# A planned graph-network kernel: layer jobs without order between units, the last two groups in alternation, and shifted ranks

## The chip, the cores and the metric

The kernel runs on one core of a Trainium2 chip. The core has a matrix engine (TensorE, PE in the profile), a vector engine (VectorE, DVE), an engine for activation functions (ScalarE, ACT), a general engine (GpSimd, POOL) and an engine that here only issues transfers (SyncE, SP). Each works through its own queue of instructions strictly in order, and an instruction waits at the head of its queue until what it needs has been signalled.

The metric is the device time of one execution in microseconds (us), as the median of several runs. Lower is better.

## What is computed

The input is 128 graphs of 64 nodes with 256 features, `x`, an integer adjacency `adj`, and a node mask of ones. Four layers follow, each of the form `x = x + layer(relu(layernorm(x)), adj)`:

```python
# 0: graph attention, 4 heads of 64:  softmax over neighbours of leaky_relu(e_src + e_dst), then elu
x = x + _L0_gnn_ref(h, adj, ...)
# 1: the same with one head of 256
x = x + _L1_gnn_ref(h, adj, ...)
# 2: relations: sum over r of (adj == r) @ ((h W + b_r) * sigmoid(h W Wg + bg_r)), then relu
x = x + _L2_gnn_ref(h, nodemask, adj, ...)
# 3: gated recurrence, three times:
m = h @ weight[i];  aggr = A^T @ m;  h = gru_cell(aggr, h)     # A = (adj != 0)
```

With edges of 0 and 1 only one of layer 2's relations can occur. The kernel computes this case in its fast part and sets a flag from the largest edge; a general part, which is not run on these inputs, stands behind that flag. All arithmetic is in 32-bit floating point. A layer of the recurrence consists of the sum over neighbours, the products for the two gates and for the candidate, `tanh` for each of them, and the new state `(1 - z) n + z h`.

## The kernel before

**Tiling.** Two graphs make one tile of 128 nodes, and four tiles make a group (`G = 4`), so there are 16 groups (`NG`). A group goes through layer 0, 1 and 2 (`first_layer`, `second_layer`, `third_layer`), and then through three steps of the recurrence. Groups 0 and 1 go through the three layers as two units of two tiles each, the other groups as one unit. In the recurrence, the state is held with features on partitions (`hT`), as two halves of 128 features (c = 0, 1), and each step multiplies it by a recursive scheme of seven products in place of eight (`Sevens`), with sums of the state (`hS`) and of the neighbour sums (`aS`) made on GpSimd. A step has 42 products of 128 by 128 by 256, each carried out in two passes of the matrix engine. The neighbour sum itself (`along`) needs the state with nodes on partitions (`hnat`) and is made of 64 by 64 products that run beside each other.

**From a step to the next.** The new state `hT` must be turned back into `hnat`. There are two ways. `back` transposes on TensorE and copies on ScalarE: this is used when the next step in the list is of the same group (`quick`), and for the last step of all (`final`). Otherwise `back_by_dma` transposes blocks of 32 on VectorE, writes them to DRAM in one transfer (tile `way`), and reads them back with four transfers; for a group's last step, `finish` then adds the result to `xg` on GpSimd and stores it.

**The order of the steps.** The list `steps` (line 1486) interleaves neighbouring groups: (g, 0), (g-1, 2), (g, 1) for each g, where (g, i) is step i of group g. It ends with (14,0), (13,2), (14,1), (15,0), (14,2), (15,1), (15,2). `when` gives every step a time slot of 27 us, from which due times of the jobs are taken, and two places ahead of a group's first step `enter` records its three layers.

**The planner.** Nothing is emitted as it is written. While `nc.on` is set, every call is recorded as an `Op` of a `Job`, with a cost from a formula (`cost`, line 529) and its dependences. `Plan.emit` (line 462) then lays all of them out in time, `PASSES` times: `forward` goes ahead in time and always takes the operation that can start earliest, or of those within a leeway the one of the lowest rank (`op.due`), on each engine; `backward` goes back from the end, and its latest starts become the ranks of the next pass, with a little noise from `SEED`. The order of the pass with the earliest end is emitted, and so becomes the order of the five queues. A job with names in `after` may not start before these jobs have ended (line 368). Buffers are taken from pools at plan time as they come free.

**Jobs that wait for jobs.** In `layers_of`, the dictionary `users` (line 1495) holds for each of the three layers the last unit that was recorded in it, and the next unit's job of that layer names it in `after` (line 1514): layer i of a unit waits for the whole of layer i of the unit before.

**Fillers.** Before the planned time of 115 us, `emit` puts matmuls on a constant tile (`warm`, line 1579) where it has planned TensorE to be idle, one for each 220 ns, as long as no bank of the recurrence has been used. Their results are not used.

**A step's end.** In `step` (line 1005), `gates` makes r and z for each c, `from_h` and `from_a` make the candidate. Each of r, z and the candidate comes in two halves of 256 columns (h = 0, 1). `z_there` applies the `tanh` to z of one c when both halves are there, and `done` makes the new state of that c in two operations of 512 columns. The last step of all is called with `in_parts`: its results are stored in three pieces.

Of the kernel before, what the change touches and what calls it, by code (L numbers as in the profile page):

```python
# [2 lines left out]

# [8 lines left out]
AF = mybir.ActivationFunctionType  # L12
# [209 lines left out]
class Plan:  # L222
# [54 lines left out]
            b.ops.append(op)  # L277
        return op

    PASSES, SEED, SPREAD = 21, 28, 50.0  # L280
    LEEWAY = {"PE": 100.0, "DVE": 100.0, "Activation": 100.0, "Pool": 100.0, "SP": 300.0, "-": 0.0}
    OVERLAP = {"DVE": 83.0, "Activation": 95.0, "Pool": 43.0}
    ISSUE, TURN = 665.0, 197.0
# [133 lines left out]
    def backward(self, end):  # L417
# [19 lines left out]
        def limit(op, late):  # L437
            if late < op.late:
                op.late = late
            op.waits -= 1  # L440
            if not op.waits:
                ready[op.engine].append(op)

        for _ in self.ops:
# [14 lines left out]
            for other in before[op]:  # L459
                limit(other, op.due - self.LATENCY - other.took)  # L460

    def emit(self):

        self.on = False
        self.link()
        best, self.random = None, Random(self.SEED)
        for _ in range(self.PASSES):
            end, order = self.forward()
            if best is None or end < best[0]:
                best = end, [(op, op.start, op.idle, op.places) for op in order]  # L470
            self.backward(end)
        self.ends = best[0]
        for op, start, idle, places in best[1]:
            op.start = start
            if op.engine == "PE" and self.spare and start < 115.0 * 1e3:
                for _ in range(int((idle - 100.0) / 220.0)):
                    self.spare()
            for b, tag in places:
                b.pool.make(b, tag)
            op.call()  # L480
        self.ops = []
        return best[0]
# [26 lines left out]
def elements(x):  # L509
    n = 1  # L510
    for k in x.shape[1:]:
        n *= k
    return n
# [15 lines left out]
def cost(engine, method, args, kwargs):  # L529

    n = elements(args[0])
    if engine == "tensor":
        m = elements(args[2] if method == "matmul" else args[0])
        return (m / 1.2 + 2.5) * (1 if method == "transpose" else 2)
    if engine == "sync" or method == "dma_start":
        to, of = args[:2]
        rate = {"way": 450.0, "fine": 175.0}.get(to.base.tag, 150.0) if isinstance(to, View) else 150.0
        if isinstance(of, View) and of.base.tag in ("way", "fine"):
            rate = 150.0 if of.base.tag == "way" else 100.0
        return n * to.shape[0] * 4 / rate  # L540
    if engine == "vector":
        if method == "bn_stats":
            return 400.0
        if method == "tensor_reduce":
            n = elements(args[1])
        plain = method == "tensor_scalar" and not any(isinstance(a, View) for a in args[2:4])
        return 150.0 + n * (0.53 if plain and n >= 512 else 1.04)
    if engine == "scalar":
        return 150.0 + 0.86 * n if method in ("copy", "mul") else 310.0 + 0.73 * n
    if ALU.pow in args:  # L550
        return 1000.0
    return 200.0 + 2.1 * n if method != "memset" else 100.0 + 0.85 * n
# [3 lines left out]
def kernel(  # L556
# [28 lines left out]
    nc = Plan(tc.nc)  # L585
    B = x.shape[0]
    NP = B * N // P
    NG = NP // G
# [26 lines left out]
    brz = nc.kept(const, [P, 4], F32, name="brz")  # L615

    def state(work, plain, name="hT"):

        return work.tile([P, K, G, P] if plain else [P, P // S, K, G * S], F32, name=name)

    def chunk(x, k):

        return x[:, k] if x.shape[1] == K else x[:, :, k]
# [301 lines left out]
    class Recurrence:  # L925
# [7 lines left out]
        def at(self, x, k, h):  # L933

            return chunk(x, k)[:, 2 * h : 2 * h + 2]
# [69 lines left out]
        def step(self, i, back=True, in_parts=False):  # L1005
# [4 lines left out]
            at = self.at  # L1010
# [45 lines left out]
            hnew = state(work, self.plain)  # L1056
            t = [[at(hnew, c, h) for h in range(2)] for c in range(K)]

            def turned_part(name):
                return work.tile([P, P // S, P], F32, name=name)  # L1060
# [18 lines left out]
            def gates(c):  # L1079
                g = Sevens(c, "r", (0, 1))  # L1080
                rs, zs = (turned_part(name) for name in "rz")
                r, z = ([x[:, 2 * h : 2 * h + 2] for h in range(2)] for x in (rs, zs))

                def r_there(h, y):
                    nc.scalar.activation(r[h], y, AF.Tanh, bias=brz[:, c : c + 1], scale=0.5)
                    nc.vector.scalar_tensor_tensor(t[c][h], r[h], 1.0, t[c][h], op0=ALU.add, op1=ALU.mult)

                def z_there(h, y):
                    nc.vector.tensor_tensor(z[h], y, z[h], ALU.add)
                    if h == 0:  # L1090
                        nc.scalar.activation(zs, zs, AF.Tanh, bias=brz[:, 2 + c : 3 + c], scale=0.5)

                nc.scalar.copy(r[0], g.mul("y", 1))
                nc.vector.tensor_tensor(r[0], g.mul("m", 2), r[0], ALU.add)
                r_there(0, r[0])
                nc.scalar.copy(z[0], g.mul("y", 6))
                nc.scalar.copy(z[1], g.mul("y", 5))
                z_there(1, g.mul("z", 7))
                r_there(1, g.mul("y", 3))
                z_there(0, g.mul("z", 4))  # L1100
                return r, z, rs, zs

            def done(d, z, to):
                nc.vector.scalar_tensor_tensor(d, z, 1.0, d, op0=ALU.add, op1=ALU.mult)
                nc.vector.scalar_tensor_tensor(to, d, 0.5, to, op0=ALU.mult, op1=ALU.add)

            def from_a(gated):
                n = Sevens(0, "n", (1,))

                def add(c, h, y):  # L1110
                    nc.vector.tensor_tensor(t[c][h], t[c][h], y, ALU.add)

                def there(c, h):
                    d, z, ds, zs = gated[c]
                    nc.scalar.activation(t[c][h], t[c][h], AF.Tanh, bias=bi[:, 4 + c : 5 + c])
                    nc.gpsimd.tensor_tensor(d[h], at(hT, c, h), t[c][h], ALU.subtract)

                add(0, 0, n.mul("y", 1))
                add(0, 0, n.mul("m", 2))
                there(0, 0)  # L1120
                add(1, 0, n.mul("y", 6))
                add(1, 1, n.mul("y", 5))
                add(1, 1, n.mul("z", 7))
                there(1, 1)
                add(0, 1, n.mul("y", 3))
                there(0, 1)
                done(*gated[0][2:], chunk(hnew, 0))
                if back:
                    back_first()
                add(1, 0, n.mul("z", 4))  # L1130
                there(1, 0)
                done(*gated[1][2:], chunk(hnew, 1))

            def back_first():
                self.hT = hnew
# [23 lines left out]
    with ExitStack() as s1:  # L1159
# [126 lines left out]
        for s in range(2):  # L1286
            h = slice(s * N, (s + 1) * N)
# [196 lines left out]
        start, slot = 87.96, 27.0  # L1484
        PLAIN = (0, NG - 1)
        steps = [(0, 0), (0, 1)]
        for g in range(1, NG):
            steps += [(g, 0), (g - 1, 2), (g, 1)]
        steps.append((NG - 1, 2))
        turn = {step: n for n, step in enumerate(steps)}  # L1490

        def when(g, i):
            return start + turn[g, i] * slot

        users = {}

        def layers_of(g):
            if g > 1:
                load_group(g)

            if g == 0:
                units = [(0, 2, (-2.5, 24.3, 61.4, 71.1)), (2, 2, (-2.7, 25.3, 58.8, 74.4))]
            elif g == 1:
                units = [(0, 2, (24.1, 54.4, 87.6, 97.3)), (2, 2, (45.5, 67.3, 90.0, 120.0))]
            elif g == 2:
                units = [(0, G, (74.5, 115.0, 160.0, 205.0))]
            else:
                end = when(g, 0) - 32.8
                units = [(0, G, [end - 51.3 * i + x for i, x in ((3, 0.0), (2, -0.95), (1, -4.68), (0, 0.0))])]
            for p0, n, at in units:  # L1510
                spare = g == 0 and p0 > 0
                for i in range(3):
                    end = None if g < 2 else at[i + 1]
                    nc.begin((g, p0, i), at[i], end, [users[i]] if i in users and not spare else [])
                    if g > 1:
                        nc.job.spread = 3.0
                    if not spare:
                        users[i] = (g, p0, i)
                    layers[i](g, p0, n, spare)
            if g == 0:  # L1520
                nc.begin("make")
                nc.note("-", make_gru, 0.0, [], [], [op for op in nc.ops if any(b.pool is early for b in op.bases)])
# [12 lines left out]
        for n, (g, i) in enumerate(steps):  # L1535
# [4 lines left out]
            at = when(g, i)  # L1540
# [259 lines left out]
```

## Time and profile before

| | |
|---|---|
| time, median of 3 runs | 1331.21 us (1329.94 to 1332.13) |
| time of the profiled execution | 1333.37 us |
| its span, from first to last instruction | 1331.6 us |
| TensorE busy | 1307.7 us, 98% |
| TensorE weight loads | 1039.4 us, 78% |
| VectorE busy | 1065.1 us, 80% |
| ScalarE busy | 859.2 us, 65% |
| GpSimd busy | 691.5 us, 52% |
| granted TensorE clock, mean | 0.993 of full |
| transfers | 143.90 MB, mean 108 GB/s |

How to read it: the profile page describes one execution. Busy time is the time in which an engine has at least one instruction at work; TensorE's matmuls are pipelined, so that a record reaches into the next one. The chain of work is followed back from the last instruction: at each step to what released it, or to the instruction before it on its engine. Groups gather the instructions of one engine, operation and shape; as nearly every call goes through the planner's one line, L495, they are told apart by the names of their tiles (`sy`, `sz`: banks of the recurrence's products; `tp`, `tq`: banks of transposes and neighbour sums; `mm`, `mn`: banks of the layers; `xg`: a group's features; `way`: the state in DRAM).

### The profile page before, as it was taken

How to read it: one execution, taken by the hardware profiler on the slowest of the kernel's cores; microseconds unless marked ns; L12 is line 12 of the kernel's file. 1: busy time of each engine (PE TensorE's matmuls, PEld its weight loads, DVE VectorE, ACT ScalarE, POOL GpSimd, SP SyncE). 2: the span in 40 equal slices, each digit the busy share in tenths (PEclk: the TensorE clock that was granted, in tenths of full speed). 3: DMA queues.
4: the chain of work that ended last, by engine and by line, in shares of the span. 5: the costliest groups of instructions: out<-in, count | busy, mean ns of one | idle time of the engine just before them, and what ended most of it. 6: DMA issues, size and time to landing. Idle time of an engine off the chain costs nothing.

```text
span 1331.6 us, 27942 instructions
## 1 busy us (share of the span) xinstructions
PE 1307.7 (98%) x9889; PEld 1039.4 (78%) x9889; DVE 1065.1 (80%) x2556; ACT 859.2 (65%) x2173; POOL 691.5 (52%) x845
## 2 busy tenths in 40 slices
PE   9998999999999999999999999999999999999986
PEld 8666877878788787878778787877878788778875
DVE  6578688897979788796988879697897979777663
ACT  4866667676676767666676666766676666655543
POOL 2664553655565355554645455654555546453642
PEclk9999999999999999999999999999999999999998
DMA  7110224435343534524253443434335323422210
GB/s 215 28 36 25 80 85 152 123 101 166 104 124 96 157 114 125 155 94 133 84 159 112 124 148 103 134 98 151 100 115 164 101 90 91 142 66 56 98 54 20
DMA packets 132061, 143.90 MB, mean 108 GB/s; under 512 B 43336, under 2 KB 117320, under 8 KB 131912
## 3 DMA queue, kind: packets, MB, share of 16 engines
q1 hardware_dynamic: 131352, 141.50, 34.8%
q8 instruction: 81, 1.33, 0.4%
q14 instruction: 68, 0.56, 0.1%
q10 hardware_dynamic: 560, 0.52, 0.1%
HBM read 80.48 MB, written 60.96 MB: 106 GB/s over the span
## 4 chain that ended last, share of the span: by engine, by line
PE 93%; DVE 3%; ACT 2%; POOL 1%; issue 0%; DMA 0%; SPq 0%; DVEq 0%; POOLq 0%
PE sy L495 37%; PE sz L495 28%; PE mm L495 17%; PE mm L787 4%; PE tp L787 3%; PE sz L1582 2%; PE tp L495 1%; DVE hT L495 1%; PE tq L787 1%; ACT hn L495 1%; DVE r L495 0%; PE mn L787 0%; DVE t L495 0%; DVE st L495 0%; ACT z L495 0%
## 5 line engine op out<-in xcount | busy, mean ns | idle before, releaser
L495 POOL TENSOR_TENSOR r<-hT,hT 128x256 f32<-128x256 f32 x192 | 152.2, 799 | 266.1 <-ACT hT L495 265.2
L495 DVE SCALAR_TENSOR_TENSOR hT<-r,hT 128x256 f32<-128x256 f32 (+1 forms) x288 | 181.6, 635 | 39.2 <-ACT r L495 37.0
L495 PE MATMUL sy<-hS,wsum 128*128 128x256 f32 x576 | 173.4, 384 | 1.0 <-ACT z L495 0.6
L495 PE MATMUL sy<-aS,wsum 128*128 128x256 f32 x576 | 173.0, 383 | 0.0
L495 PE MATMUL sz<-hS,whh 128*128 128x256 f32 x576 | 170.5, 383 | 0.1
L495 PE MATMUL sz<-aS,wc 128*128 128x256 f32 x576 | 164.7, 383 | 0.0
L495 DVE TENSOR_TENSOR hT<-hT,sz 128x256 f32<-128x256 f32 x288 | 118.2, 411 | 54.7 <-PE sz L495 48.3
L495 POOL TENSOR_TENSOR aS<-aT 128x256 f32<-128x256 f32 x96 | 80.9, 843 | 150.8 <-ACT aT L495 150.6
L495 ACT ACTIVATE hT<-sy,bh 128x256 f32<-128x256 f32 x192 | 90.6, 472 | 68.8 <-PE sy L495 66.4
L495 PEld LDWEIGHTS sy<-hS,wsum 128*128 128x128 f32 x576 | 107.1, 191 | 30.3 <-issue 8.8
L495 ACT ACTIVATE hT<-hT,bi 128x256 f32<-128x256 f32 x192 | 95.3, 505 | 50.9 <-DVE hT L495 49.5
L495 PEld LDWEIGHTS sz<-hS,whh 128*128 128x128 f32 x576 | 107.1, 190 | 23.2 <-issue 7.4
L495 PEld LDWEIGHTS sy<-aS,wsum 128*128 128x128 f32 x576 | 107.2, 190 | 19.7 <-issue 3.2
L495 PEld LDWEIGHTS sz<-aS,wc 128*128 128x128 f32 x576 | 106.5, 190 | 18.4 <-issue 1.2
L495 POOL TENSOR_TENSOR rstd<-var,mhalf 128x4 f32<-128x4 f32 (+1 forms) x70 | 74.9, 1070 | 82.6 <-ACT var L495 78.1
L495 PE MATMUL mm<-wl,hT 128*128 128x512 f32 x248 | 117.5, 593 | 0.0
L495 ACT ACTIVATE hn<-xg,nm,rstd 128x256 f32<-128x256 f32 x200 | 107.2, 593 | 10.7 <-POOL nm L495 10.2
L495 ACT COPY z<-sy 128x256 f32<-128x256 f32 x192 | 70.7, 369 | 66.4 <-PE sy L495 65.0
L495 DVE TENSOR_TENSOR hT<-hT,sy 128x256 f32<-128x256 f32 x192 | 79.6, 414 | 32.6 <-PE sy L495 30.2
L495 DVE TENSOR_TENSOR z<-sz,z 128x256 f32<-128x256 f32 x192 | 79.7, 416 | 32.3 <-PE sz L495 27.5
L495 DVE SCALAR_TENSOR_TENSOR r<-z,r 128x512 f32<-128x512 f32 x96 | 89.0, 929 | 13.8 <-ACT z L495 7.6
L495 DVE BATCH_NORM_STATS2 st<-xg 128x6 f32<-128x256 f32 x256 | 95.8, 409 | 3.2 <-DMA xg<-in_x_dram 3.1
(207 smaller groups left out, 3228.7 us busy)
## 6 DMA issues: line engine op xcount, KB each, us to landing
way<-tb SPq DMA_DIRECT2D x58, 512.0 KB, 2.7
hnat<-way SPq DMA_DIRECT2D x180, 128.0 KB, 2.9
way<-hn SPq DMA_DIRECT2D x42, 512.0 KB, 3.0
hn<-way SPq DMA_DIRECT2D x168, 128.0 KB, 3.0
xg<-in_x_dram SPq DMA_DIRECT2D x15, 512.0 KB
out_dram<-xg SPq DMA_DIRECT2D x15, 512.0 KB, 2.9
t<-row SPq DMA_DIRECT2D x28, 256.0 KB, 4.0
hT<-way SPq DMA_DIRECT2D x52, 128.0 KB, 2.6
```

What stands on the lines that cost most here:

```text
L495: return do(*[real(a) for a in args], **{k: real(v) for k, v in kwargs.items()})
L787: nc.nc.tensor.matmul(*[real(x) for x in product], start=True, stop=True)
L1582: nc.spare = lambda: psum.spare and nc.nc.tensor.matmul(pause, warm, warm, start=True, stop=True)
```

## The change

Six things are edited.

1. `users` is gone: a layer's job no longer names the job of the unit before.
2. The end of the list of steps becomes (14,0), (13,2), (15,0), (14,1), (15,1), (14,2), (15,2). Only (0,0), (0,1) still follow each other directly, so (15,1) now goes back by DMA.
3. In the last step of all, `tanh` of z and `done` work on halves of 256 columns, one after each half.
4. The planner's rates for transfers from `way` go from 150 to 170, and those for a tag `fine` from 175 to 220 and from 100 to 125.
5. There are 27 passes in place of 21, with another seed.
6. After the passes, the ranks with which the best pass began are shifted by job: each number in `MOVES` seeds a generator that picks a place in time and a width, and shifts the ranks of about half of the jobs there, on all engines alike or on each by itself. One more `forward` with these ranks gives the order that is emitted.

```diff
-    PASSES, SEED, SPREAD = 21, 28, 50.0
+    PASSES, SEED, SPREAD = 27, 39, 50.0
+    MOVES = (
+        10, 12, 18, 24, 27, 28, 58, 71, 83, 84, 89, 99, 118, 129, 136, 141, 144, 198, 214, 221, 266, 299, 322, 324,
...
+    )
...
+    RANKED = ("PE", "DVE", "Activation", "Pool", "SP")
+
+    def move(self, seed, end, jobs):
+
+        x = seed * 0x9E3779B97F4A7C15
+
+        def u():
+            nonlocal x
+            x = (x * 6364136223846793005 + 1442695040888963407) % 2**64
+            return (x >> 11) * 2.0**-53
+
+        def shift(by):
+            return math.floor(by * (u() + u() + u() - 1.5) * 2.0 + 0.5)
+
+        u()
+        middle = u() * end
+        width = (15e3 if u() < 0.5 else 50e3) * (0.3 + u())
+        by = (60.0, 200.0, 600.0, 2000.0)[int(u() * 4)]
+        together = int(u() * 3) == 0
+        for j in jobs:
+            if not abs(j.sum / j.count - middle) < width or u() < 0.5:
+                continue
+            if together:
+                d = shift(by)
+                for e in self.RANKED:
+                    j.shift[e] += d
+            else:
+                for e in self.RANKED:
+                    if u() >= 0.5:
+                        j.shift[e] += shift(by)
...
         for _ in range(self.PASSES):
+            ranks = [op.due for op in self.ops]
             end, order = self.forward()
             if best is None or end < best[0]:
-                best = end, [(op, op.start, op.idle, op.places) for op in order]
+                best = end, ranks, [op.start for op in self.ops]
             self.backward(end)
+        end, ranks, starts = best
+        jobs = list({id(op.job): op.job for op in self.ops}.values())
...
+        for m in self.MOVES:
+            self.move(m, end, jobs)
+        for op, due in zip(self.ops, ranks):
+            op.due = due + op.job.shift.get(op.engine, 0.0)
+        end, order = self.forward()
+        best = end, [(op, op.start, op.idle, op.places) for op in order]
...
-        rate = {"way": 450.0, "fine": 175.0}.get(to.base.tag, 150.0) if isinstance(to, View) else 150.0
+        rate = {"way": 450.0, "fine": 220.0}.get(to.base.tag, 150.0) if isinstance(to, View) else 150.0
         if isinstance(of, View) and of.base.tag in ("way", "fine"):
-            rate = 150.0 if of.base.tag == "way" else 100.0
+            rate = 170.0 if of.base.tag == "way" else 125.0
...
                     nc.vector.tensor_tensor(z[h], y, z[h], ALU.add)
-                    if h == 0:
+                    if in_parts:
+                        nc.scalar.activation(z[h], z[h], AF.Tanh, bias=brz[:, 2 + c : 3 + c], scale=0.5)
+                    elif h == 0:
                         nc.scalar.activation(zs, zs, AF.Tanh, bias=brz[:, 2 + c : 3 + c], scale=0.5)
...
                     nc.gpsimd.tensor_tensor(d[h], at(hT, c, h), t[c][h], ALU.subtract)
+                    if in_parts:
+                        done(d[h], z[h], t[c][h])
...
-        for g in range(1, NG):
+        for g in range(1, NG - 1):
             steps += [(g, 0), (g - 1, 2), (g, 1)]
-        steps.append((NG - 1, 2))
+        steps[-1:] = [(NG - 1, 0), (NG - 2, 1), (NG - 1, 1), (NG - 2, 2), (NG - 1, 2)]
...
-                    nc.begin((g, p0, i), at[i], end, [users[i]] if i in users and not spare else [])
+                    nc.begin((g, p0, i), at[i], end)
```

## The prediction

> **What bounds the kernel now.** The page gives TensorE 98% busy, 24 us idle in all. The chain that ended last is 93% TensorE, 1.9% of it the filler matmuls of line 1582, which compute nothing. So I asked for busy time by stages, cut where the clock or the load changes; the columns after the stage are its length and the busy us (instructions) of each engine.
>
> ```profile
> 0.00:115.00 115.00, 112.17 (x798) 84.31 (x799) 76.48 (x220) 73.37 (x226) 53.22 (x96) 1.00 0.32 88
> 115.00:147.00 32.00, 27.80 (x302) 21.20 (x302) 25.68 (x66) 21.02 (x48) 21.00 (x26) 0.95 0.10 35
> 147.00:1292.00 1145.00, 1142.12 (x8626) 912.91 (x8625) 945.51 (x2239) 751.48 (x1872) 605.12 (x709) 1.00 0.38 115
> 1292.00:1303.00 11.00, 7.39 (x74) 5.73 (x76) 5.45 (x8) 4.11 (x8) 6.38 (x8) 0.69 0.15 49
> 1303.00:1332.00 29.00, 18.25 (x109) 15.22 (x98) 12.03 (x26) 9.19 (x20) 5.79 (x8) 0.83 0.08 23
> ```
>
> The middle, 1145 us, has 2.9 us of TensorE idle: nothing of size can be gained there without less matmul work, and the change takes none away. What can be gained lies in four places: the fillers, 115 to 147, 1292 to 1303, and the tail. The groups by form show the fillers (212 records, two passes for each of 106 instructions):
>
> ```profile
> L1582 PE MATMUL sz<-warm 128*128 128x128 f32 x212 | 29.3, 289 | 1.1 <-DVE warm L1580 1.1
> ```
>
> The waits of TensorE name the other two, and the order in time places them:
>
> ```profile
> PE tp L495 <- DVE hT L495: 9.9, 5, 3.6
> ```
>
> ```profile
> 1291.64 1.03 PE L495 MATMUL sz<-aS,wc 128*128 128x256 f32 x4
> 1296.28 1.09 PE L495 MATMUL tp<-ident,hT 128*128 128x128 f32 x4 [3.61 <-DVE hT L495]
> 1297.16 1.91 PE L495 MATMUL sy<-hT,whh 128*128 128x256 f32 x4
> 1298.87 1.06 PE L495 MATMUL tp<-ident,hT 128*128 128x128 f32 x4
> ```
>
> These are the steps (15,1) and (15,2), the only pair besides (0,0),(0,1) that runs with nothing between: TensorE waits for the new state, transposes it itself, and then four passes take 1.71 us (1297.16 to 1298.87) where four take 0.86 at full clock. At (0,0),(0,1) VectorE and GpSimd show why the state is late:
>
> ```profile
> 128.07 1.42 DVE L495 SCALAR_TENSOR_TENSOR hn<-hn,o 128x1024 f32<-128x1024 f32 x1
> 129.52 1.10 DVE L495 SCALAR_TENSOR_TENSOR r<-z,r 128x512 f32<-128x512 f32 x1
> ...
> 130.88 2.50 DVE L495 SCALAR_TENSOR_TENSOR hT<-r,hT 128x512 f32<-128x512 f32 x1
> ```
>
> ```profile
> 130.04 2.79 POOL L495 TENSOR_TENSOR xg<-xg,hn 128x1024 f32<-128x1024 f32 x1
> ```
>
> An attention operation stands between the operations of the state, and the last, 0.69 us elsewhere, takes 2.50 beside GpSimd's 2.79.
>
> **The Trainium skill.** TensorE: Matmul & The Clock Gate, section What's actually happening: after about 3.4 us of idling in a free-running window TensorE runs at half clock until it has been busy as long. The trace agrees: clock 0.69 in the stage with the 3.8 us hole. Perfetto Trace Analysis, section Identifying the Most-Contended Engine, says that matmul busy share is no measure of headroom because matmuls are pipelined; here each record reaches some 0.17 us past the next one's start, so I count gaps from start to start. GPSIMD Engine Reference, section Specifications: GpSimd shares its memory interface with VectorE operations that have two inputs there; the 2.50 us agrees.
>
> **The change part by part.** Instruction counts are from the built programs.
>
> Fillers: 84 instead of 106, all ahead of the first recurrence product. The planner places one for each 220 ns in which it expects TensorE idle (before 115 us), so they count its idle; in the chain 12 of them (x24) take 2.68 us, 0.223 each: 22 x 0.223 = 4.9 us less. This is the end of "users": groups 1 and 2 may start a layer while the unit before is still in it, and more attention (the order has the aggregates and two of group 2's products earlier) stands before the first recurrence product. Not below 0 us gained unless the fillers gone leave bare holes; 4.9 is taken.
>
> (0,0) to (0,1): today the last product ends at 126.67 and TensorE idles 1.29, 0.69 and 2.66 us, 4.6 in all, before the second four transposes at 133.52. Then passes and 64x64 products run slow until 138.1: 0.3 + 0.6 + 0.8 = 1.7 us. In the new order eight attention products (258 or 264 columns, 0.44 each, 3.5 us) stand between the last product and the first transposes, and one more before the second: 3.5 + 0.45 + 0.86 + 0.44 = 5.3 us of cover. On VectorE the four state operations stand together, with neither the 1.42 us operation nor statistics between, and GpSimd's add of the attention is ahead. Today's 6.7 us less 1.42, 0.41, 0.41 and 1.81 is 3.1 us needed. Gain 4.6 + 1.7 = 6.3; bounds 2 (another collision on the port) and 6.3. I take 6.0.
>
> The end: the order becomes (15,0), (14,1), (15,1), (14,2), (15,2). Today 1292.50 to 1302.28, 9.8 us, holds ten passes (10 x 0.216 = 2.2 us) and eight transposes. The transposes go (48 to 40 in the program), and the state goes through memory: one more write and four more reads, two more VectorE transposes. That path is measured one step earlier: last product of (15,0) at 1255.06, write issued 1260.06, reads 1262.71 to 1264.4 and 2.9 to land: 1267.3, 12.3 us. In the new order the products between the last of (15,1) and the neighbour sums of (15,2) are about 37 of (14,2), 37 x 0.43 = 16 us, and (14,1) to (14,2), (15,0) to (15,1) have a whole step, 18 us, too. Hidden with 4 us to spare; without that cover it would cost its 12.3. Gain 9.8 - 2.2 = 7.6. Group 15 must then be ready one step earlier. The sixteen copies of its start are the tight place (issued on SyncE from 1215.9 to 1227.1; GpSimd, waiting for them, starts at 1228.75, and TensorE's first product is at 1229.50): between its last relation product and that use there are 28 us of TensorE work in the new order, 27 in the old, so no wait either way. Queued behind those issues is the write of (14,0), which has until (14,1), 19 us after. GpSimd's add for group 14's output (2.37 us) stands before the last step's four subtractions; it may hold them by 1 us.
>
> The tail: the last pass ends at 1319.4, the last sum at 1324.4, the span at 1331.6. Halves instead of wholes: after the last product one z addition 0.42, a tanh of about 0.5 instead of 0.71, and 2 x 0.42 instead of two pairs of 0.69 on VectorE, partly waiting for the transposes. By the new queue order the last sum ends some 3.9 us after the last pass instead of 5.0; the outputs leave staggered. Gain 1.0, bounds 0 and 2.
>
> The shifted ranks and the new DMA rates (170 and so on; no tile carries the tag "fine") emit no instruction. They decide the order in the middle. Runs of 64x64 products, whose entry and exit cost 0.2 us a pair by start to start, are 133 instead of 132: 0.2 lost. The work between an exponentials' transpose and its aggregate, which covers the row's two DMAs, is at least 8.2 us with one head in both orders. For the middle I bound between +2.9 (all idle gone) and -5 and take a loss of 1.5.
>
> Sum: 4.9 + 6.0 + 7.6 + 1.0 - 0.2 - 1.5 = 17.8 us. The profiled execution took 1333.4 (span 1331.6, about 1.8 around it), so 1315.6; the median, 1331.2, is 2.2 below that execution: 1313.4.
>
> **The rivals.** A: only the end is gained (7.6 + 1.0), the start meets other holes: the planner's expectations there are less true (today 7 us of gaps stand beside the fillers before the first recurrence product). 1331.2 - 8.6 = 1322.6, less with part of the start, so 1319 to 1324. B: new holes in the middle eat all. It is one mechanism: SyncE's queue is in order, and a layer's row or state read that the shifted ranks place behind another unit's waiting write lets TensorE wait at each of 14 groups. At 1.3 us a group it makes 18 and decides the sign; at 2 us, 28 - 18 = +10: 1341. Against it: equal distances above, the DMA share of 0.38, 2.9 us idle today. C: the alternation doesn't hide, because (15,0) waits for its sixteen copies; 4 us of cover short of 12.3 leaves a gap with a cold clock of up to 8: about 1321. D: no change to be measured (within 0.2%, 2.7 us): needs gains and losses to cancel.
>
> **How the numbers follow.** Likeliest case 0.68, at 1313.4, its own range 1308 to 1318.5; A 0.16; C 0.06; B 0.07; D 0.03. The range that leaves out B, D, the far half of A's upper end and a gain over 24 is 1306.5 to 1323. Faster by over 0.2% 0.90, within 0.02 (some of D), slower 0.08. 0.2% is about what a measurement of this kernel can tell.
>
> **What would show it.** Right: no wait of TensorE over 1 us after 1270, transposes of hT 40; full clock at 115 to 147 and at the last but one step; fillers 168 records; the first neighbour sums of (0,1) some 10 us earlier for the same work. Wrong: TensorE idle above 5 us in the middle, waits for hT by DMA at (15,0), or half clock in the first 150 us.

## The result, and the profile after

The changed kernel takes 1316.98 us (median of 5 runs, 1316.05 to 1317.70), the kernel before 1330.83 (5 runs, 1329.94 to 1332.13): ratio 0.9896, 95% interval 0.9882 to 0.9911, 13.9 us less. Predicted were 1313.4 us and a range of 1306.5 to 1323.0: the sign and the range hold, the point is 3.6 us too low.

Busy time by stages of the changed kernel; after the stage come its length and the busy us (instructions) of TensorE, its weight loads, VectorE, ScalarE and GpSimd, then granted clock, DMA share and GB/s:

```profile
0.00:115.00 115.00, 112.04 (x836) 80.89 (x837) 89.45 (x280) 82.23 (x257) 59.35 (x101) 1.00 0.43 119
115.00:147.00 32.00, 31.85 (x270) 26.70 (x270) 23.89 (x58) 23.48 (x61) 20.75 (x26) 1.00 0.13 38
147.00:1275.00 1128.00, 1125.28 (x8541) 897.85 (x8540) 921.66 (x2176) 735.57 (x1823) 601.91 (x706) 1.00 0.37 113
1275.00:1303.00 28.00, 27.16 (x183) 23.04 (x181) 18.26 (x39) 14.17 (x31) 11.58 (x12) 1.00 0.24 76
1303.00:1315.00 12.00, 2.60 (x13) 1.53 (x12) 5.00 (x13) 1.15 (x3) 0.72 (x1) 0.76 0.17 52
```

The middle of the kernel before, cut at the same times:

```profile
147.00:1275.00 1128.00, 1125.12 (x8547) 898.02 (x8546) 934.21 (x2214) 744.29 (x1856) 598.29 (x702) 1.00 0.38 116
```

The stage 115 to 147 had 4.2 us of TensorE idle at clock 0.95; it has 0.15 at 1.00. The hole near 1292 with clock 0.69 is gone. The middle idles 2.7 us, 2.9 before.

The groups by form, the fillers and the transposes of the state:

```profile
L1638 PE MATMUL sz<-warm 128*128 128x128 f32 x168 | 24.5, 294 | 1.1 <-DVE mhalf L549 1.1
L549 PE MATMUL tp<-ident,hT 128*128 128x128 f32 x16 | 2.8, 279 | 1.9 <-DVE hT L549 1.9
```

168 records are 84 fillers, as counted. The 16 transposes (24 before) are those after the first and after the last step: (15,1) to (15,2) needs none now. Their idle before fell from 9.9 us to 1.9. What TensorE waits for, total, times, longest:

```profile
PE tp L549 <- DVE hT L549: 1.9, 3, 1.2
PE sy L549 <- DVE hT L549: 1.4, 1, 1.4
...
PE sz L549 <- DVE hT L549: 0.8, 1, 0.8
...
PE sz L549 <- DVE z L549: 0.6, 1, 0.6
```

The first row is in the tail, the second at 1222.66 us. The last two are new and lie in the last step. In order of time, where the third comes from:

```profile
1296.69 2.36 POOL L549 TENSOR_TENSOR xg<-xg,hnat 128x1024 f32<-128x1024 f32 x1 [5.79 <-DMA hnat<-way]
...
1297.19 0.42 DVE L549 TENSOR_TENSOR hT<-hT,sy 128x256 f32<-128x256 f32 x1 [0.41 <-PE sy L549]
...
1297.52 1.80 DVE L549 SCALAR_TENSOR_TENSOR hT<-r,hT 128x256 f32<-128x256 f32 x1
...
1299.71 0.48 PE L549 MATMUL sz<-aS,wc 128*128 128x256 f32 x1 [0.84 <-DVE hT L549]
```

GpSimd's addition for the output of group 14 runs beside a VectorE operation that takes 0.42 us elsewhere; it takes 1.80, and a product waits for it.

**Where the time went.** I counted from each matmul's start to the next one's, less its pitch (0.216 us for 256 columns, 0.109 for 128), and call an excess of over 0.15 us a wait; passes at half clock count in it too. The stages are cut by TensorE's work without fillers, so that they hold the same work in every kernel: its first 90 us, the next 15 (they hold (0,0) to (0,1)), up to 1203, the rest. The last five columns are us of one profiled execution each; fillers count from each one's start to the next matmul's. e1 to e12 are the experiments of the next section. "Planned" is the end that the kernel's own planner expects; it enters the kernel only as what the planner minimises. Ratios are to runs of the kernel before on the same chip.

| kernel | ratio (95%) | planned | fillers | waits, first 90 | (0,0) to (0,1) | middle | end |
|---|---|---|---|---|---|---|---|
| before | 1 | 1319.8 | 27.2 | 2.4 | 5.5 | 3.9 | 8.7 |
| after | 0.9896 (0.9882 to 0.9911) | 1300.8 | 21.8 | 3.2 | 0.0 | 4.2 | 4.2 |
| e3 step order only | 0.9989 (0.9982 to 0.9996) | 1322.1 | 28.8 | 0.9 | 5.6 | 6.0 | 3.3 |
| e5 no waits of jobs only | 1.0000 (0.9990 to 1.0011) | 1318.9 | 26.7 | 0.8 | 0.0 | 8.6 | 8.1 |
| e12 the same in groups 1 to 3 | 0.9960 (0.9948 to 0.9973) | 1317.5 | 28.2 | 0.9 | 0.2 | 4.8 | 8.7 |
| e2 all structure | 1.0005 (0.9996 to 1.0014) | 1317.2 | 28.4 | 3.4 | 1.3 | 12.1 | 4.1 |
| e4 passes, seed, rates only | 1.0009 (1.0000 to 1.0018) | 1319.9 | 28.2 | 0.0 | 4.7 | 4.8 | 8.7 |
| e1 after without shifts | 0.9942 (0.9923 to 0.9960) | 1311.9 | 25.4 | 4.1 | 0.7 | 8.0 | 3.8 |
| e10 after, 80 of 123 shifts | 0.9935 (0.9914 to 0.9957) | 1305.0 | 25.1 | 2.7 | 0.0 | 6.9 | 4.3 |
| e11 jobs wait, own shifts | 0.9987 (0.9975 to 0.9999) | 1312.9 | 28.0 | 0.8 | 6.1 | 7.0 | 4.5 |
| e9 before, own shifts | 0.9963 (0.9948 to 0.9978) | 1314.1 | 26.5 | 1.8 | 4.5 | 2.9 | 7.9 |
| e7 hole filled | 0.9986 (0.9978 to 0.9994) | order of before | 26.9 | 2.2 | 5.7 | 3.2 | 3.4 |
| e8 addition in pieces | 0.9900 (0.9885 to 0.9915) | order of after | 21.9 | 3.2 | 0.0 | 5.5 | 3.2 |

Two executions of one order (before and e7, after and e8) differ by 0.7 and 1.3 us in the middle; there, differences below that say nothing. From before to after: fillers -5.4, step -5.5, end -4.5, first 90 us +0.8, middle within that noise.

### The profile page after: what moved, and what is told of

The parts are those of the page before. It is cut to its first block, busy times and chain, and to the rows that moved or that the text cites. A ratio compares the mean times of both kernels' runs of the same rounds, so it can differ in the third digit from the quotient of the medians.

```text
span 1314.2 us, 27889 instructions
## 1 busy us (share of the span) xinstructions
PE 1298.9 (99%) x9837; PEld 1030.0 (78%) x9837; DVE 1058.3 (81%) x2562; ACT 856.6 (65%) x2173; POOL 694.3 (53%) x845
## 4 chain that ended last, share of the span: by engine, by line
PE 85%; DVE 5%; ACT 5%; POOL 2%; issue 1%; DMA 1%; SPq 0%; ACTq 0%; DVEq 0%; POOLq 0%
PE sy L549 34%; PE sz L549 25%; PE mm L549 15%; PE mm L841 3%; PE tp L841 3%; ACT hn L549 2%; DVE hT L549 2%; PE sz L1638 1%; PE tp L549 1%; DVE t L549 1%; ACT hT L549 1%; PE tq L841 1%; DVE r L549 1%; POOL rstd L549 1%; DVE st L549 1%
## 5 line engine op out<-in xcount | busy, mean ns | idle before, releaser
L549 POOL TENSOR_TENSOR r<-hT,hT 128x256 f32<-128x256 f32 x192 | 156.2, 820 | 274.9 <-ACT hT L549 273.6
L549 PEld LDWEIGHTS sz<-aS,wc 128*128 128x128 f32 x576 | 106.9, 190 | 17.8 <-DVE hT L549 1.2
L549 POOL TENSOR_TENSOR rstd<-var,mhalf 128x4 f32<-128x4 f32 (+1 forms) x70 | 78.1, 1115 | 77.0 <-ACT var L549 76.8
L549 DVE TENSOR_TENSOR z<-sz,z 128x256 f32<-128x256 f32 x192 | 79.5, 415 | 28.7 <-PE sz L549 27.2
L549 POOL TENSOR_TENSOR hS<-hT 128x256 f32<-128x256 f32 x96 | 80.0, 834 | 38.1 <-DMA hT<-way 15.2
```

The costliest lines, as they stand in the source:

```text
L549: return do(*[real(a) for a in args], **{k: real(v) for k, v in kwargs.items()})
```

## The experiments

The theory T was the forecast's: four places add up, and each part of the change brings its own. Against it: R1, the search over shifted ranks brought most of it; R2, any new plan moves the time by several us either way. A plan is the order that the planner emits; nearly every edit brings a new one.

**The parts alone.** Undoing the shifts in the changed kernel:

```diff
-    MOVES = (10, 12, 18, ... 24055, 25299)
+    MOVES = ()
```

> The changed kernel without the list of shifted ranks (MOVES empty); step order, halves, passes, seed and rates stay. The plan comes out with 97 fillers instead of 84. Theory T (the gain lies in four places: fillers about 5 us, the step (0,0) to (0,1) about 6, the hole before the last step 7.6, the tail 1 to 2.6; the list of shifts only trims the fillers): 13 fillers x 0.223 = 2.9 us are lost, so 1317 + 2.9 = about 1320, with full clock at 115 to 147 and before the last step. Rival R1 (the search over shifts brought most of it, as it also tuned the middle): the middle shows more than 4 us of new TensorE idle and the time is 1326 or more. Rival R2 (any new plan moves the time by several us, either way): 1313 to 1330, with differences in stages that the list does not touch by its purpose.

1324.35 us, 7.4 above the changed kernel; T had 1320, R1 1326 or more. Fillers account for 3.6 us, a little over T's 2.9; the middle's waits for another 3.8, which T did not have.

Structure without the new plan settings (the kernel before, with its own passes, seed and rates):

```diff
-        for g in range(1, NG):
+        for g in range(1, NG - 1):
             steps += [(g, 0), (g - 1, 2), (g, 1)]
-        steps.append((NG - 1, 2))
+        steps[-1:] = [(NG - 1, 0), (NG - 2, 1), (NG - 1, 1), (NG - 2, 2), (NG - 1, 2)]
...
-    nc.begin((g, p0, i), at[i], end, [users[i]] if i in users and not spare else [])
+    nc.begin((g, p0, i), at[i], end)
...
+    if in_parts: ...   # tanh, additions, subtractions in halves in the last step
```

> The kernel before with the three edits of structure (units no longer wait for each other as jobs, new step order, halves in the last step), with the old passes, seed and rates and without shifted ranks: 105 fillers. T: the hole before the last step goes (-7.6), the tail loses 1 to 2.6, the step (0,0) to (0,1) gains up to 6 because its order is the new one, fillers as before (-0.2): 1331 - 15 = 1316 to 1319. R1: only the end is gained, and the middle loses: 1322 to 1327. R2: the start or the middle is off by several us in places without a change of order: above 1327.

1332.11: no gain at all. The two holes go (-4.2 and -4.6 us), and the middle's waits rise by 8.2, fillers by 1.2, waits of the first 90 us by 1.0. One wait of the middle is for the sixteen copies that group 15 starts from:

```profile
PE sy L495 <- DMA hT<-tb: 1.8, 1, 1.8
```

It is 0.9 in e1 and absent in the changed kernel: a small form of the forecast's rival C. T's total falls here, its places do not.

The step list alone (the first hunk above):

> The kernel before with the new step list only. 117 fillers instead of 106, so 11 x 0.223 = 2.5 us are lost at the start; the order at (0,0) to (0,1) stays the old one. T: the hole before the last step and its half clock go, -7.6, the tail stays at about 12.2 us after the last pass: 1331 + 2.5 - 7.6 = 1326, and full clock in the last step. Rival C (the alternation does not hide the state's path through memory): at the steps (15,1) and (15,2) TensorE waits for hT by DMA, 1331 or more.

1330.03. The hole before the last step and its cold clock are gone (end -5.4), TensorE waits nowhere for the state by DMA: rival C, as put here, falls. But the plan that comes with it has 1.6 us more fillers and 2.1 more waits in the middle, and T's 1326 is missed.

Passes, seed and rates alone:

```diff
-    PASSES, SEED, SPREAD = 21, 28, 50.0
+    PASSES, SEED, SPREAD = 27, 39, 50.0
...
-        rate = {"way": 450.0, "fine": 175.0} ... 150.0 ... 100.0
+        rate = {"way": 450.0, "fine": 220.0} ... 170.0 ... 125.0
```

> The kernel before with the new passes, seed and rates only (no list of shifts, no edit of structure): 106 fillers as before. T: the four places stay as they were, half clock at (0,0) to (0,1) and before the last step, so 1331, give or take 2. R2 (any new plan moves the time by several us): outside 1328 to 1334, and then the other runs are to be compared stage by stage and not by their totals.

1332.09: both holes stay, so the settings bring nothing on the old structure. On the new one (e2 to e1) the same settings with the same structure are worth 0.6%. With one plan on each side, this can be a plan's luck as well as something in the settings; which was not shown.

The free layers alone (the second hunk above):

> The kernel before with one edit: the list of users is gone, so that layers of different units no longer wait for each other as jobs (old step order, old halves, no shifted ranks). 103 fillers instead of 106. The forecast's step by step working: fillers -0.7, the hole at (0,0) to (0,1) with its half clock -6.0, rest unchanged: about 1324. Rival theory from the runs with structure only and order only, that fillers and gaps of the start are one budget (before 27.2 + 10.8 = 38.0 us, structure only 28.4 + 8.9 = 37.3, order only 28.8 + 10.0 = 38.9): the hole goes, but the attention that now covers it is missing where it was, as fillers or gaps: start 36.5 to 38.5 in all, the middle gains some us of gaps as in the run with structure only (+6), the end stays as before: 1330 to 1337.

1330.61: the total came as the rival had it, 6.6 us above T's 1324. Its cause did not. The theory of one budget is wrong: fillers and waits of the first 105 us fell from 35.1 to 27.5 us, a little more than T said; all of that was lost again in the middle, where T had no change. The step (0,0) to (0,1) loses all its waits:

```profile
115.00:147.00 32.00, 32.00 (x277) 26.79 (x276) 24.17 (x61) 22.75 (x61) 17.32 (x21) 1.00 0.21 59
147.00:1275.00 1128.00, 1121.96 (x8509) 891.01 (x8508) 937.56 (x2167) 731.67 (x1816) 599.52 (x700) 1.00 0.37 112
```

The first row is full, where the kernel before has 27.80 of 32. The second shows the payment: 6.0 us idle instead of 2.9 (1125.12 busy of 1128), and 4.7 us more waits by starts. They lie in 18 places (6 before) and are up to 1.05 us long; the list of waits puts 3.5 us down to ScalarE and 1.9 to VectorE.

Is it the later groups' freedom that costs? Free in groups 1 to 3 alone:

```diff
-    ... [users[i]] if i in users and not spare else [])
+    ... [users[i]] if i in users and not spare and g >= 4 else [])
```

> The kernel before, with layers of different units free of each other for the groups 1 to 3 alone; from group 4 on they wait as before (old step order, halves, passes, seed and rates, no shifts). 107 fillers; attention products stand between (0,0) and (0,1). Theory U (without the waits the start gains its 5.7 us at that step, and the middle loses because the later groups' layers may run into each other): the step has no wait left, the middle's waits of TensorE stay at the 3 to 4 us of the kernel before: 1331 - 5.7 + 0.2 = 1325.5. Rival V (the middle's loss is what any plan has that has not been searched, wherever it is free): the step has no wait left, and the middle shows 7 us of waits or more: 1329 to 1332.

1326.13, as U had it. The same two stages:

```profile
115.00:147.00 32.00, 31.83 (x269) 26.31 (x268) 23.46 (x58) 22.96 (x60) 18.99 (x23) 1.00 0.18 55
147.00:1275.00 1128.00, 1125.38 (x8541) 897.11 (x8540) 931.94 (x2198) 738.17 (x1835) 605.24 (x709) 1.00 0.37 114
```

The start's gain stays and the middle is that of before. It is one plan against one plan, so it speaks for U more than it proves it; that the new structure with the wait kept from group 4 on would beat the changed kernel was not tried.

**Search against structure.** A list of shifts of its own for the kernel before:

```diff
+    MOVES = (4, 21, 54, 64, 72, ...)   # 76 shifts, applied as in the changed kernel
```

> The kernel before, nothing of its structure changed (units wait for each other, old step order, old halves, passes, seed and rates), with a list of shifted ranks of its own: 76 shifts, kept from 7848 tried because each lowered the end that the planner expects (1319.8 us without them, 1314.1 with). 101 fillers. In the changed kernel a fall of 11.1 us in the planner's expectation (no shifts to all shifts) brought 7.4 us on the chip, 0.66 of it. R1 (the search does it, on any structure): 1331 - 0.66 x 5.7 = 1327 or less. Rival (structure first: the old barrier and the hole before the last step leave the search nothing to collect): within 1.5 us of 1331.

1326.37, 4.9 us less: the search works on the old structure too, and R1 is right to that extent. The two holes stay (4.5 and 7.9): the search cannot take them.

The changed kernel with an equally long search:

```diff
-    MOVES = (10, 12, ... 7602, 7657, 7774, ... 25299)
+    MOVES = (10, 12, ... 7602, 7657, 7774)
```

> The changed kernel with only those of its shifts whose numbers are up to 7848 (80 of 123), so that it has had as long a search as the kernel beside it: the planner expects 1305.0 us instead of 1300.8. 91 fillers. By the same 0.66: 1317 + 2.8 = 1319.8. If the shifts work through single lucky places, anything from 1317 to 1324.

1322.74, 2.9 above the expectation: 5.8 above the kernel with all shifts, and 1.6 below the one without, which the intervals can't tell from none. The factor 0.66 from planned to measured time holds for no single step.

And with the waits of jobs put back, and a search of the same length for it:

```diff
-    MOVES = (10, 12, ... 25299)
+    MOVES = (4, 12, 27, ... 7429)   # 86 shifts
...
-    nc.begin((g, p0, i), at[i], end)
+    nc.begin((g, p0, i), at[i], end, [users[i]] if i in users and not spare else [])
...
+    if not spare:
+        users[i] = (g, p0, i)
```

> The changed kernel with one edit undone, layers of different units wait for each other as jobs again, and with a list of shifts of its own found in as many trials (86 kept from 7848; the planner expects 1312.9 us, 109 fillers). Beside the run with the short list this is the worth of that edit under equal search. T (the edit brings the start, fillers and the step (0,0) to (0,1)): 5 to 7 us slower than the short list, about 1325 to 1327, with a hole of 3 to 5 us again between (0,0) and (0,1). Rival (the edit as such is worth nothing, as its run alone against the kernel before seemed to say): 1320, like the short list.

1329.92, 7.2 above the short list (planned: 7.9 above). The stage of the step shows why:

```profile
115.00:147.00 32.00, 27.55 (x297) 20.82 (x296) 22.73 (x67) 21.58 (x49) 18.56 (x24) 0.89 0.07 22
```

27.55 us busy and half clock again. Waits of 6.1 us at that step in place of 0.0, fillers 28.0 in place of 25.1, and 1.9 less in the first 90 us: in this pair, given the same search, the free layers are worth 7 us. In all seven kernels in which they wait this step has 4.5 to 6.1 us of waits, in all six in which they don't, 0.0 to 1.3.

Three kernels with equally long searches ran on the same chip, and together they say less for the structure. e9, with nothing of it, takes 1326.37; e10, with all of it and the new settings, 1322.74, every run below every run of e9; e11, with the new step order, halves and settings but with the waits, 1329.92, slower than e9. So a search of a given length can end several us better or worse, and the 7 us are one draw.

What is left of the theories: T's places hold, each in its own experiment, but its sum holds only with a plan that suits. R1 and R2 both have a part: on the same structure, new settings (e2 to e1) moved the time by 7.8 us and the shifts (e1 to after) by 7.4. Of the 13.9 us, the structure and settings brought 3.6 over the old kernel where both had the shorter search. The changed kernel's list comes from a longer one (numbers up to 25299); the kernel before was not given that, so how much of the 13.9 us it could have had from search alone is open.

**Single mechanisms.** Halves in the last step alone (third hunk of e2):

> The kernel before with one edit: the last step's tanh, additions and subtractions in halves. 114 fillers instead of 106 (+1.8 us). The hole before the last step stays. The forecast's tail: the last sum some 3.9 us after the last pass instead of 5.0, end of the span 1.0 nearer to the last pass (12.2 us before, so about 11.2); with the 9.6 us of the changed kernel, if halves do all of that: 9.6. Read from the trace, the time of the whole is about 1332 either way.

One run, 1330.92. The last sum ends 4.24 us after the last pass; 4.90 before, 3.87 in the changed kernel. Halves with this plan make two thirds of that gain. They do not make it by themselves: without halves the same distance is 4.55 us in e4 and 5.45 in e3, with halves 5.12 in e2, which is longer than before. From e3 to e2 halves bring 0.3, from before to e6 0.7; the rest is the order on VectorE.

The cold clock by itself; the hole is filled with matmuls that compute nothing that is used:

```diff
+    for _ in range(16):
+        nc.nc.tensor.matmul(real(to), real(ident), real(ident), start=True, stop=True)
+    nc.nc.tensor.transpose(real(to), real(of), real(ident))
...
```

> The kernel before, its plan and order unchanged, with 16 filler matmuls of 128x128 by 128 columns, 3.6 us, in front of the first transpose between (15,1) and (15,2), where TensorE idles 3.8 us. They compute nothing that is used. If the half clock after the hole costs what the forecast took (four passes 1.71 us instead of 0.86, and more until 1301.9), the clock stays full and 2 to 3 us go: 1328.5. If the passes there were slow for another reason, or the fillers end late and hold the transposes: 1331, or up to 1332.

```profile
1291.53 3.73 PE L960 MATMUL tp<-ident 128*128 128x128 f32 x32
1295.23 0.33 PE L961 MATMUL tp<-ident,hT 128*128 128x128 f32 x1
1295.40 0.49 PE L495 MATMUL tp<-ident,hT 128*128 128x128 f32 x3
1295.72 1.03 PE L495 MATMUL sy<-hT,whh 128*128 128x256 f32 x4
```

1328.92: 1.9 us less (ratio 0.9986, 0.9978 to 0.9994), with the idle time still spent. The transposes come 3.70 us after the last product where they came 3.78 after it, and the four passes behind them are busy 1.03 us instead of 1.91. So of the hole's cost 3.8 is idle time and about 2 the clock after it. The Trainium skill (TensorE: Matmul & The Clock Gate, What's actually happening) has the clock drop after an idle window of about 3.4 us. In the trace of the kernel before it drops sooner, at 1295.10, 2.6 us after the last product; more on this at the end.

GpSimd's addition for group 14 in four pieces:

```diff
-    nc.gpsimd.tensor_tensor(to, to, of, ALU.add)   # for group 14 alone
+    for p in range(G):
+        nc.nc.gpsimd.tensor_tensor(
+            real(to[:, 2 * p : 2 * p + 2]), real(to[:, 2 * p : 2 * p + 2]), real(of[:, 2 * p : 2 * p + 2]), ALU.add)
```

> The changed kernel, its plan and order unchanged, with GpSimd's addition for the output of group 14 (2.36 us in one piece of 1024 columns) in four pieces of 256 columns. If that addition holds up the last step's VectorE operation (1.80 us instead of 0.42 elsewhere) and so the last passes (waits of 0.84 and 0.63 us), VectorE gets in between two pieces, the first wait falls to 0.3 or less and the time by 0.5 to 1.2 us: about 1316.2. If the two share the port at half speed each whatever the size, or the four pieces cost more than one, no change or up to 0.5 us worse.

```profile
1298.27 0.42 DVE L549 SCALAR_TENSOR_TENSOR hT<-r,hT 128x256 f32<-128x256 f32 x1
...
1298.83 3.00 POOL L1061 TENSOR_TENSOR xg<-xg,hnat 128x256 f32<-128x256 f32 x4 [6.01 <-DMA hnat<-way]
...
1299.45 0.42 DVE L549 SCALAR_TENSOR_TENSOR hT<-r,hT 128x256 f32<-128x256 f32 x1
```

The cause of that wait is shown: the operation beside the pieces takes 0.42 us, the wait of 0.84 is gone and the end's waits fall by 1.0. The wait for z (0.63 above) stays, so the addition is not its cause. The median, 1316.80, is 0.2 below the changed kernel's, which five runs can't tell from none; the pieces cost 3.00 us instead of 2.36, with nothing behind them that waits.

## Why the prediction was right, and where not

The range held and the places named are where the time went; the sum was too high. That fillers and middle came out near their forecast is in part luck, since the reasons given for them were not, or not alone, the ones at work.

**Fillers, -4.9: right in size, half right in cause.** 84 of them, 5.4 us less. The prediction put them down to the end of `users`. The free layers alone take 106 to 103, all structure to 105; with the new settings 97, with 80 shifts 91, with all 84. So the shifts, of which it said that they "emit no instruction", place the work that the fillers stand in for. But they don't do it alone either: with the layers waiting, an equally long search leaves 109 (e11) where it leaves 91 with the layers free (e10).

**(0,0) to (0,1), -6.0: right.** Waits 5.5 to 0.0 and full clock. The first neighbour sums of (0,1) start at 136.4 us, 136.1 before, but now with 8.9 us more of work done ahead of them, where the prediction had some 10. The cause is the named one, and e5, e11 and e12 isolate it. One sum was off without consequence: 6.7 less 1.42, 0.41, 0.41 and 1.81 is 2.65, not 3.1.

**The end, -7.6: too much by 2.0.** The hole and its cold clock went, and the alternation hid the state's path through memory. Without the waits among the tail's transposes the end went from 5.7 us of waits to 1.8, small gaps gave 0.9 and the eight transposes 0.8: 5.6 in all. The 1.8 that are left are new. By starts, 1.0 of it is the wait beside GpSimd's addition. The prediction named this addition ("it may hold them by 1 us") and left it out of the sum, but it meant the last step's four subtractions, which stand behind it in GpSimd's queue. Those were not held: GpSimd idled before the first of them. The other 0.8 is the wait for z 4 us later.

```profile
1300.28 0.73 POOL L549 TENSOR_TENSOR r<-hT,hT 128x256 f32<-128x256 f32 x1 [1.23 <-ACT hT L549]
...
1303.63 0.70 PE L549 MATMUL sz<-hS,whh 128*128 128x256 f32 x2 [0.63 <-DVE z L549]
```

What was held was a VectorE operation. The prediction had read just such a collision at (0,0) to (0,1), and did not count one here. "No wait over 1 us after 1270" holds up to the last passes; in the tail one of 1.2 is left.

**The tail, -1.0: right in size.** The last sum ends 3.87 us after the last pass instead of 4.90, and the span 5.5 us after that sum. Before it was 7.1, but 5.8 in e7, which has the same order: SyncE's last issue of the output took 2.48 us in the one execution and 0.48 in the other. Taken against e7, the tail's gain is 1.3: 1.0 before the last sum, as predicted, and 0.3 after it, where executions with a short last issue scatter by more (5.1 to 6.5 us). The cause named, halves, is only a part of it (e2, e6).

**Switches and middle, +0.2 and +1.5: near in sum, wrong in reasoning.** Where runs of 64x64 products begin and end there are 253 short gaps before and 254 after; the middle's waits are 4.2 and 5.5 us in two executions after, 3.9 and 3.2 before. The prediction took this as what the shifts would cost. The runs show the opposite: the free structure brings 5 to 8 us of waits with an unsearched plan (e5, e2), and settings and shifts took most of it back. Rival B was real as a danger, since e2 stands at 1.0005, but mostly not through SyncE's queue: of e2's 12.1 us in the middle, the wait for copies that SyncE issues is 1.8. Rival A, a start that gains nothing, did not come: fillers and step gave 11.2 us where 10.9 were forecast, less 1.3 in the first 90 us.

**Not in the sum:** waits of the first 90 us, from 2.4 to 3.2, and small gaps there, 0.5. Why they grew stays open.

The parts measured make 5.4 + 5.8 + 5.6 + 1.3 - 1.3 - 0.9 = 15.9 us (fillers, step with its small gaps, end, tail, first 90 us, middle as the mean of two executions each) where the forecast had 17.8: 1.9 of the 3.6 us. The rest lies between single executions and medians. The forecast took before's profiled execution as 2.2 us above its median and carried that over to the changed kernel. It is 2.5 above the median of five, and the changed kernel's is 0.9 below its own. The distance is no property of profiling: 1.3 of it is that one issue, and the execution had a granted clock of 0.993, at which eight of 39 runs of the kernel before average 1332.4, with 1330.9 as the median of all (one chip, e1's runs). The changed kernel, without the two holes, has 0.997 to 0.999 in every run.

## What to carry to other kernels

Where a planner orders everything, an edit brings its own stage's gain and a new draw of all the others. Here the step order alone, the free layers alone and all structure together came out between 0.1% faster and nothing, with the holes they aimed at gone. Judge such an edit by its stage, and its total only with the same search for both sides, better with several searches. Where an ordering rule costs at one place, lift it at that place first: here this kept 5.3 us of the gain (e12) that lifting it everywhere lost (e5), with one plan each.

## What the runs showed that was not expected

- The clock fell without 3.4 us of idling in one piece. In all fourteen traces it changes only at whole multiples of 3.413 us from its first change. I cut the traces into these stretches and counted TensorE's idle time in each from start to start. The 27 stretches at full clock with 2.15 to 3.25 us idle were all followed by half clock; of some 5300 others, with 2.08 us or less, none was. At (0,0) to (0,1) in the kernel before, no single idle time was over 2.66 us. So here about 2.1 us of idling within one stretch were enough, and where a hole lies in that grid decides as well as its length.
- The times of the kernel before go with the clock granted: 39 runs on one chip lie between 1336.1 us at 0.991 and 1328.0 at 0.998, 0.85 us for each 0.001 in a straight-line fit. That its holes meet the grid differently from run to run would explain it, and was not shown.
- The last output issue on SyncE took 0.37 to 0.48 us in most profiles and 2.48, 2.25 and 1.63 in three (before, e6, e9), and the span of these ended 7.1 to 7.4 us after the last sum instead of 5.1 to 6.5. A tail should be read from more than one profile.
- A GpSimd addition of 1024 columns (2.36 us) stretched a VectorE operation from 0.42 to 1.80 us; it ended 0.28 us after the addition. Beside four additions of 256 columns (3.00 us together) it took 0.42, and the addition that it met 0.94 instead of 0.73. The Trainium skill (GPSIMD Engine Reference, Specifications) has GpSimd share its memory interfaces with VectorE, with contention for VectorE operations that have two inputs there. The trace agrees: `hT<-hT,sy`, with one input from TensorE's bank, took its 0.42 beside the long addition. Both traces fit an interface that is held for a whole instruction, so that shorter ones let the other engine in; each shows it for one operation.
- The planner's expectation fell by 19.0 us from before to after and the time by 13.9; between e10 and after 4.2 planned gave 5.8, between e1 and e10 6.9 gave 1.6.
